# Token layer of a four-layer convolution network: a chunk's pieces in another order, its means in another PSUM bank

## The chip, the cores and the metric

The kernel runs on one core of a Trainium2 chip. The metric is the device time of one launch in microseconds; the median of three runs is 7043.77 us (7041.89 to 7046.84). The core has five engines that work side by side, each through its own queue of instructions in order: TensorE (PE; its weight loads are listed as PEld), VectorE (DVE), ScalarE (ACT), GpSimd (POOL) and SyncE (SP), which mostly issues DMAs. TensorE writes its products to PSUM, which has eight banks.

## The reference, cut to what matters

The input x has shape (4, 48, 256, 256). Four residual layers follow each other; each first normalizes x in 16 groups of channels (`_gn`) and adds its result to x.

```
x = x + L0(_gn(x))   # channel attention: 1x1 and 3x3 depthwise convolutions, softmax over 48x48, projection
x = x + L1(_gn(x))   # the token layer
x = x + L2(_gn(x))   # scans with a 5-tap convolution: down, up, right, left
x = x + L3(_gn(x))   # the same with other weights
```

The token layer reads the normalized image as tokens of 48 numbers, by a plain reshape of memory:

```
t = x.reshape(B, H * W, dim)
t = gelu(gelu(t @ W1 + b1))               # 48 -> 16, exact gelu, twice
x1, x2 = t[..., :8], t[..., 8:]
n = layernorm(x2)                         # mean and variance over 8 numbers
sp = depthwise3x3(n) + dw_b;  ch = conv1x1(n) + pw_b     # n as an image with 8 channels
g = x1 * (sp * ch)
out = g @ W2 + b2                         # 8 -> 48
```

## The kernel before, in words

`layers01` computes layers 0 and 1, `scans` layers 2 and 3. In `layers01` a first stage sums the products from which the attention of each image is made. Then the output of layer 0 is computed in blocks of 16 rows, 16 blocks an image. `block(u)` has six pieces, three to a half block: two calls of `full` (three matmuls each) and one of `rest` (six matmuls on two halves of the rows at once). Half block 0 takes the parts c = 0 and 2, half block 1 the parts 1 and 3. `rest` ends with two additions on VectorE (L720) and two `bn_stats` (L721), which collect the statistics for the next normalization; at half block 1 it also lets ScalarE normalize the next block's input (x1n and x2n, L654). The function `conv` runs one half block.

The 16 blocks of image 0 run alone. The remaining 96 half blocks share the engines with the token layer: four of them run first, and then `tick(c, conv, alone)` (L1040) is called once for each step of the token layer, which is cut into 32 chunks of 32 rows (eight an image). A tick holds four half blocks and pieces of three chunks: the transposes of chunk c + 1, the hidden layer and the norm of chunk c, gate and output of chunk c - 2. When no half blocks are left, `alone` is true and the ticks hold token work only; that is so from chunk 22 on. In the text these are lone ticks, the others mixed ticks.

The pieces of a chunk, in the order in which its data needs them:

- `load` and `relay` (L860, L867): the tokens come by DMA (tok), and GpSimd rearranges them in two copies (pairs).
- `transposed` (L873): six pieces, each four transposes on TensorE into one bank and a copy out of it (xt), by VectorE for even pieces and ScalarE for odd ones.
- `hidden` (L820, L890 to L901): two groups of eight matmuls, each into one bank, and the gelus on ScalarE.
- `centered` (L907 to L911): a matmul gives the mean in every row (pm), VectorE subtracts it (d), GpSimd squares (sq).
- `normed` (L916 to L942): a matmul gives the variance (pvar); ScalarE takes the root, VectorE the reciprocal (L919) and the product (L921), ScalarE writes n (L923). Four small DMAs on ScalarE's queue then carry border rows: two of the chunk itself (L933, L934), one into the border tile of the chunk before (L938), one into that of the chunk after (L942). At an image's first or last chunk one of them carries zeros.
- `shift` and `gate` (L946 to L961): GpSimd copies the border tile three times, shifted (nears). TensorE makes the depthwise convolution (psp): three matmuls from n (L952) and one from the border copies (L953); another matmul makes the pointwise convolution (pch, L955). ScalarE and VectorE combine the two (sp), GpSimd multiplies (g).
- `output` (L991 to L1006): for each of two parts ip, four matmuls into four banks (pout), eight additions of the residual on VectorE (L1001) into y, eight copies on GpSimd into yr. `finish` takes four `bn_stats` of y (L1034). One DMA pair writes yr to memory for the scans (x2r, L1018).

The PSUM banks are five in the pool `banks`, two in `spare` and one in `p_small`. The tiles of `banks` are handed out in rotation: a tile waits until the fifth tile before it has been read. Half block 0 uses `spare`, half block 1 `banks`; everything else named above uses `banks`.

The program is written with a tile framework: the Python code gives an order of pieces, and a planner with estimated costs puts the instructions of each engine's queue in an order that may differ from it a little. On each engine the built order is kept at run time. In a mixed tick of the kernel before, TensorE's built order is: mean, two of the six transposing pieces, projections of part 0, half block 1, two transposing pieces, variance, projections of part 1, half block 0, two transposing pieces, half block 1, hidden layer of the next chunk, gate, half block 0.

## Time and profile before

| what | us |
|---|---|
| median of three runs | 7043.77 |
| the profiled execution, its own time | 7044.79 |
| span of its instructions | 7042.9 |
| first mean of a chunk / mean of chunk 22 / mean of chunk 31 (start) | 1221.8 / 2323.9 / 2614.5 |
| first work of the scans | 2697.2 |
| one mixed tick without a disturbance, 1406.4 to 1456.2 | 49.8 |

| busy in the whole span | us |
|---|---|
| TensorE matmuls | 6623.6 |
| VectorE | 3630.5 |
| GpSimd | 2085.2 |
| ScalarE | 1854.1 |

A row of the timeline has the start, the time until the group's last instruction ends, the engine (with a q when it is the engine's queue issuing a DMA), the line, the operation, out<-in, and how often; in square brackets the idle time of the engine before it and what ended it. Matmuls of 32-bit numbers stand as two records each. A busy TensorE can contain waits that are shorter than a record, so the distance from one group's start to the next is the better measure. The granted clock is the share of TensorE's full clock.

### The profile page before, as it was taken

Reading aid. Unit: us, or ns where it says so; the run is one execution under the profiler, and the core shown is the slowest. Engines: PE = TensorE matmul, PEld = TensorE weight load, DVE = VectorE, ACT = ScalarE, POOL = GpSimd, SP = SyncE. Lnnn points to the kernel's source line nnn. Section 1 sums busy time; section 2 is a strip of 40 time slices with the busy share of each in tenths; the row PEclk is TensorE's granted clock in tenths of the full one; section 3 lists DMA queues with packets and bytes.
Section 4 is the critical chain, followed back from the end, with each engine's and each line's share of the span. In section 5 each row is a group of like instructions: output and inputs, shape, how many; then the busy total and the mean of one; then the engine's idle time right before and its main releaser. Section 6 shows DMA issues by size and latency. Waiting matters only on the chain.

```text
span 7042.9 us, 133633 instructions
## 1 busy us (share of the span) xinstructions
PE 6623.6 (94%) x55772; PEld 5308.8 (75%) x55772; DVE 3630.5 (52%) x8740; ACT 1854.1 (26%) x2166; POOL 2085.2 (30%) x4211
## 2 busy tenths in 40 slices
PE   6999999999999767999998999986898999899999
PEld 5666533333333226999998999986798999899999
DVE  7777533455555554444444446754344444444444
ACT  3430022434344443453431000001444444000000
POOL 0000000233333454330003556762000000455777
PEclk9999999999999888999999999998899999999999
DMA  7742145666666667994677777989997466865775
GB/s 233 183 133 83 62 142 165 180 176 186 182 190 185 158 156 218 294 282 122 207 210 186 202 185 174 253 241 196 179 170 126 140 191 182 227 191 173 275 292 202
DMA packets 1177470, 1326.23 MB, mean 188 GB/s; under 512 B 831040, under 2 KB 1005760, under 8 KB 1124512
## 3 DMA queue, kind: packets, MB, share of 16 engines
q1 hardware_dynamic: 1163696, 1229.16, 64.3%
q10 hardware_dynamic: 13072, 88.18, 3.7%
q8 instruction: 438, 7.18, 0.4%
q14 instruction: 168, 1.38, 0.1%
q0 software_dynamic: 96, 0.33, 0.0%
HBM read 794.28 MB, written 522.19 MB: 187 GB/s over the span
## 4 chain that ended last, share of the span: by engine, by line
PE 56%; SPq 3%; DMA 3%; DVE 2%; POOL 1%; issue 1%; ACT 1%; ACTq 0%; POOLq 0%; DVEq 0%
PE ps L1206 55%; SPq L1242 3%; DMA D<-d 1%; ACT d L1281 1%; POOL s L1491 1%; DMA near<-n 0%; DMA tok<-x 0%; DVE y L1001 0%; DVE v L919 0%; POOL yr L1006 0%; DVE st L1034 0%; DMA r<-R 0%; DMA x2r<-yr 0%; PE ptok L873 0%; PE ph L820 0%
## 5 line engine op out<-in xcount | busy, mean ns | idle before, releaser
L1206 PE MATMUL ps<-d,w 128*128 128x128 f32 (+1 forms) x18360 | 2075.3, 277 | 107.7 <-DVE d L1212 69.4
L1206 PEld LDWEIGHTS ps<-d,w 128*128 128x128 f32 x18360 | 2070.6, 193 | 112.3 <-DVE d L1212 73.0
L1206 PE MATMUL ps<-r,w 128*128 128x128 f32 (+1 forms) x18360 | 2066.5, 276 | 69.8 <-POOL r L1423 36.5
L1206 PEld LDWEIGHTS ps<-r,w 128*128 128x128 f32 x18360 | 2064.2, 193 | 72.1 <-POOL r L1423 37.4
L1212 DVE SCALAR_TENSOR_TENSOR d<-ps,b,d 128x128 f32<-128x128 f32 x3054 | 978.6, 348 | 1166.1 <-PE ps L1206 1080.3
L1491 POOL TENSOR_TENSOR s<-s,r 128x128 f32<-128x128 f32 x1536 | 748.3, 528 | 330.3 <-DVE r L1212 327.8
L1212 DVE SCALAR_TENSOR_TENSOR r<-ps,b,pre 128x128 f32<-128x128 f32 x1530 | 490.4, 348 | 578.9 <-PE ps L1206 569.2
L1212 DVE SCALAR_TENSOR_TENSOR r<-ps,b,r 128x128 f32<-128x128 f32 x1530 | 489.2, 347 | 458.8 <-PE ps L1206 430.5
L374 PE MATMUL acc<-moving,raw 128*32 128x240 f32 (+1 forms) x6144 | 688.9, 382 | 12.2 <-DVE moving L357 11.5
L697 PE MATMUL py<-x1n,wy 128*96 128x512 f32 x1536 | 696.7, 602 | 1.9
L1423 POOL COPY pre<-c 128x128 f32<-128x128 f32 x1530 | 559.5, 405 | 464.7 <-DVE r L1212 463.7
L374 PE MATMUL acc<-moving,still 128*32 128x240 f32 (+1 forms) x6144 | 685.5, 382 | 6.0 <-DVE still L361 2.2
L1281 ACT ACTIVATE d<-x,spread 128x256 f32<-128x256 f32 x752 | 510.6, 826 | 555.5 <-DMA D<-d 343.5
L1362 ACT COPY u<-d 128x384 f32<-128x384 f32 x510 | 452.0, 903 | 569.9 <-DVE d L1212 509.4
L374 PEld LDWEIGHTS acc<-moving,raw 128*32 128x32 f32 x6144 | 434.9, 110 | 197.6 <-DVE moving L357 11.8
L697 PEld LDWEIGHTS py<-x1n,wy 128*96 128x96 f32 x1536 | 243.7, 164 | 415.1 <-issue 373.4
L1423 POOL COPY r<-c 128x128 f32<-128x128 f32 x6 | 2.4, 396 | 1700.1 <-DMA c<-U 1700.1
L720 DVE TENSOR_TENSOR y<-py,t 96x512 f32<-96x512 f32 x256 | 173.3, 677 | 559.6 <-PE py L706 559.6
L374 PEld LDWEIGHTS acc<-moving,still 128*32 128x32 f32 x6144 | 361.2, 110 | 37.0 <-issue 5.8
L1006 POOL COPY yr<-y 96x256 f32<-96x256 f32 x512 | 316.1, 660 | 202.0 <-DVE y L1001 191.8
L706 PE MATMUL py<-x2n,wy 64*96 64x512 f32 x1536 | 362.5, 604 | 0.0
L706 PEld LDWEIGHTS py<-x2n,wy 64*96 64x96 f32 x1536 | 117.0, 159 | 234.4 <-issue 229.5
(219 smaller groups left out, 4173.9 us busy)
## 6 DMA issues: line engine op xcount, KB each, us to landing
t<-in_xc SPq DMA_DIRECT2D x64, 1536.0 KB
c<-U SPq DMA_DIRECT2D x348, 256.0 KB
D<-d SPq DMA_DIRECT2D x54, 1536.0 KB
d<-D SPq DMA_DIRECT2D x54, 1536.0 KB
R<-r SPq DMA_DIRECT2D x54, 1536.0 KB
r<-R ACTq DMA_DIRECT2D x54, 1536.0 KB
U<-u SPq DMA_DIRECT2D x84, 768.0 KB
raw<-in_xp SPq DMA_DIRECT2D x36, 1728.0 KB
```

The source lines that it names most:

```text
L374: nc.tensor.matmul(out[32 * i : 32 * i + 32, : n * C], lhsT=still[i][:, first : first + 32], rhs=moving[:, i, lo : lo + n * C], start=u == ...
L697: nc.tensor.matmul(ps, lhsT=held["w"][0][:, dx], rhs=x1n[:, 2 * c : 2 * c + 2, dx : dx + W], start=dx == 0, stop=False)
L706: nc.tensor.matmul(held["ps"][q + 2 * s], lhsT=held["w"][1][here, dx], rhs=x2n[here, 2 * q : 2 * q + 2, dx : dx + W], start=False, stop=dx ...
L720: nc.vector.tensor_add(part, held["ps"][c], t1[:P, 2 * c : 2 * c + 2, :])
L1006: nc.gpsimd.tensor_copy(yrs[c][:, :, 2 * i2 + ip, :].rearrange("p j (n a g) -> p j n a g", a=4, g=4)[:, :, :, al], y[:, i2, al].rearrange( ...
L1206: nc.tensor.matmul(ps[m][:, here], lhsT=w[:, n, :], rhs=old[:, q, there], start=first, stop=last)
L1212: nc.vector.scalar_tensor_tensor(new[:, m], ps[m], bias[:, m : m + 1], inp[:, m], ALU.add, ALU.add)
L1242: queues[q % len(queues)].dma_start(v[p0 : p0 + np_, m, 8 * n0 : 8 * n1], src[c0:c1, 8 * n0 : 8 * n1, at : at + 64])
L1281: pin(nc.scalar.activation(dst, src, AF.Identity, bias=g[:, 1:2], scale=g[:, 0:1]))
L1362: nc.scalar.copy(v[:, :, i, :, al], line)
L1423: nc.gpsimd.tensor_copy(dst[:, m].rearrange("p (J a b) -> p J a b", J=NBK, b=B), v[:, m, j, :, gl].rearrange("p J b a -> p J a b"),)
L1491: nc.gpsimd.tensor_add(v, v, line[:, m].rearrange("p (J a b) -> p J a b", J=NBK, b=B))
```

## The change

In `layers01`, the `bn_stats` of a half block are put into a list and issued at the start of the next half block. The pool `big` and the pool `spare` are handed to `gated_layer`. The mean and the variance (pm, pvar) of a chunk are made in the bank of `p_small`. `normed` is split: the root stays in it, the reciprocal, the product, n and the border DMAs become `scaled`. `output` is split in two pieces of two projections each; in lone ticks the second and fourth projection use `spare`, and y of part 1 has its own buffers in `big`. In lone ticks the DMA of yr is issued in the tick's last piece instead of right after the output.

The pieces of a tick have a new order. In mixed ticks the six transposing pieces stand together behind the second half block, and the variance stands behind the third. TensorE's built order there is: mean, projections of part 0, half block 1, six transposing pieces, half block 0, variance, projections of part 1, half block 1, hidden layer of the next chunk, gate, half block 0. In lone ticks the gate comes after four transposing pieces rather than at the start, and both parts of the output come last.

On ScalarE the built order of a mixed tick has n, the normalization of x1n, and then the four border DMAs; before, the border DMAs followed n directly. On GpSimd, in lone ticks, the border copies of chunk c - 1 stand in tick c: in ticks 25, 27 and 29 ahead of the pairs copies, in ticks 26, 28 and 30 ahead of the yr copies; before, they stood at the start of tick c + 1. On SyncE, the load of tok for every second lone chunk stands behind the four loads of xr.

```
@@ -674,6 +674,7 @@
     stats = {}
     ends = []
     unwritten = []
+    behind = []
 
     def block(u):
 
@@ -683,6 +684,9 @@
         held = {}
 
         def full(c):
+            if c < 2:
+                while behind:
+                    behind.pop(0)()
             if c == 0:
                 if u + 1 < len(items):
                     ahead_[u + 1] = load(items[u + 1])
@@ -718,9 +722,15 @@
             for c in (q, q + 2):
                 part = held["y"][:, 2 * c : 2 * c + 2, :]
                 nc.vector.tensor_add(part, held["ps"][c], t1[:P, 2 * c : 2 * c + 2, :])
-                nc.vector.bn_stats(stats[b][:, n * 4 + c, :], part.rearrange("p h w -> p (h w)"))
+                behind.append(
+                    lambda c=c, part=part: nc.vector.bn_stats(
+                        stats[b][:, n * 4 + c, :], part.rearrange("p h w -> p (h w)")
+                    )
+                )
             if q == 0:
                 return
+            while behind and n == NB - 1:
+                behind.pop(0)()
             dst = x1[b].rearrange("c (h w) -> c h w", w=W)
 
             def write(y=held["y"]):
@@ -746,7 +756,7 @@
         some_late()
     sctx.close()
 
-    tick, n_ticks = gated(ctx, tc, banks, p_small)
+    tick, n_ticks = gated(ctx, tc, banks, p_small, big)
     todo = [(u, q) for u in range(NB, len(items)) for q in range(2)]
     made = {}
 
@@ -768,7 +778,7 @@
             piece()
 
 
-def gated_layer(ctx, tc, banks, p_small, x1, x2r, w1, w2, dw, ends, pw, cols, b2, k, coef1, coef2):
+def gated_layer(ctx, tc, banks, p_small, big, spare, x1, x2r, w1, w2, dw, ends, pw, cols, b2, k, coef1, coef2):
 
 
 
@@ -902,7 +912,7 @@
             h2s[c] = h
 
     def centered(c):
-        pm = banks.tile([128, CH], F32, tag="bank", name="pm")
+        pm = p_small.tile([128, CH], F32, tag="small", name="pm")
         h2 = h2s.pop(c)
         nc.tensor.matmul(pm, lhsT=k["mean8", 128], rhs=h2, start=True, stop=True)
         d = ds[c] = feat.tile([128, CH], F32, tag="d", name="d")
@@ -910,12 +920,18 @@
         sq = sqs[c] = feat.tile([128, CH], F32, tag="sq", name="sq", bufs=1)
         nc.gpsimd.tensor_mul(sq, d, d)
 
+    vs = {}
+
     def normed(c):
-        b, j = items[c]
-        pv = banks.tile([128, CH], F32, tag="bank", name="pvar")
+        pv = p_small.tile([128, CH], F32, tag="small", name="pvar")
         nc.tensor.matmul(pv, lhsT=k["mean8", 128], rhs=sqs.pop(c), start=True, stop=True)
         v = feat.tile([128, CH], F32, tag="v", name="v", bufs=1)
         nc.scalar.activation(v, pv, AF.Sqrt, bias=eps)
+        vs[c] = v
+
+    def scaled(c):
+        b, j = items[c]
+        v = vs.pop(c)
         nc.vector.reciprocal(v, v)
         d = ds.pop(c)
         nc.vector.tensor_mul(d, d, v)
@@ -975,30 +991,35 @@
         t = xrs[c, ip]
         nc.scalar.activation(t, t, AF.Identity, bias=b2_sb)
 
-    def output(c, ip, alone):
+    def output(c, ip, i, alone):
         b, j = items[c]
-        if ip == 0:
+        if ip == 0 and i == 0:
 
             yrs[c] = res.tile([P, 8, 4, 128], F32, tag="yr", name="yr")
             if j == 0:
                 stats[b] = feat.tile([P, NJ * 8, 6], F32, tag="st", name="st1")
-        y = ys[c, ip] = res.tile([P, 2, 4, W], F32, tag="y1", name="y1")
-        t, g = xrs[c, ip], gs[c]
-        ps = []
-        for q in range(4):
-            p = banks.tile([P, 2, W], F32, tag="bank", name="pout")
+        if i == 0:
+            if alone and ip:
+                ys[c, ip] = big.tile([P, 2, 4, W], F32, tag="y", name="y1", bufs=2)
+            else:
+                ys[c, ip] = res.tile([P, 2, 4, W], F32, tag="y1", name="y1")
+        y, t, g = ys[c, ip], xrs[c, ip], gs[c]
+        ps = {}
+        for q in (2 * i, 2 * i + 1):
+            ps[q] = (spare if alone and q % 2 else banks).tile([P, 2, W], F32, tag="bank", name="pout")
             here = slice(32 * q, 32 * q + 32)
             nc.tensor.matmul(
-                p,
+                ps[q],
                 lhsT=w2_sb[here, ip, :],
                 rhs=g[here],
                 start=True,
                 stop=True,
             )
-            ps.append(p)
-        for q in range(4):
+        for q in ps:
             for kk in range(2):
                 nc.vector.tensor_add(y[:, q % 2, 2 * kk + q // 2, :], ps[q][:, kk], t[:, 4 * kk + q, :])
+        if i == 0:
+            return
         if alone:
             load_x(c + 1, ip)
         for i2 in range(2):
@@ -1021,8 +1042,6 @@
                 )
 
         unwritten.append(write)
-        if alone:
-            unwritten.pop()()
 
     after = []
     unwritten = []
@@ -1062,36 +1081,30 @@
         def last():
             if c + 2 < n:
                 load(c + 2)
+            while alone and unwritten:
+                unwritten.pop(0)()
 
         pieces = [first]
         if now:
             if items[c][1] == 0:
                 pieces.append(lambda: strips(items[c][0]))
             pieces += [lambda: hidden(c, 1), lambda: hidden(c, 0)]
-        if was:
-            pieces.append(lambda: gate(old))
-        pieces.append(conv)
-        if now:
-            pieces.append(lambda: centered(c))
-        if new:
-            pieces += [lambda i=i: transposed(c + 1, i) for i in range(2)]
-        if was:
-            pieces += [lambda: [add_b2(old, ip) for ip in range(2)], lambda: output(old, 0, alone)]
-        pieces.append(conv)
-        if new:
-            pieces += [lambda i=i: transposed(c + 1, i) for i in range(2, 4)]
-        if was:
-            pieces.append(lambda: finish(old, 0))
-        if now:
-            pieces.append(lambda: normed(c))
-        if was:
-            pieces.append(lambda: output(old, 1, alone))
-        pieces.append(conv)
-        if new:
-            pieces += [lambda i=i: transposed(c + 1, i) for i in range(4, NI)]
-        if was:
-            pieces.append(lambda: finish(old, 1))
-        pieces += [conv, last]
+        turned = lambda *which: [lambda i=i: transposed(c + 1, i) for i in which] if new else []
+        out = lambda ip: [lambda i=i: output(old, ip, i, alone) for i in range(2)] if was else []
+        of_now = lambda f: [lambda: f(c)] if now else []
+        of_old = lambda f, *more: [lambda: f(old, *more)] if was else []
+        added = of_old(lambda c: [add_b2(c, ip) for ip in range(2)])
+        if alone:
+            pieces += [conv] + turned(0, 1) + of_now(centered) + turned(3) + of_old(gate) + added
+            pieces += turned(4) + of_now(normed) + turned(2, 5) + of_now(scaled)
+            pieces += out(0) + of_old(finish, 0) + out(1) + of_old(finish, 1)
+        else:
+            pieces += of_old(gate)
+            pieces += [*added, conv, *of_now(centered), *out(0), conv]
+            pieces += turned(0, 1, 3, 4, 2, 5) + of_old(finish, 0)
+            pieces += [conv, *of_now(normed), *out(1), conv]
+            pieces += of_now(scaled) + of_old(finish, 1)
+        pieces.append(last)
         if c == n + 1:
             pieces.append(lambda: [piece() for piece in unwritten + after])
         return pieces
@@ -1612,10 +1625,10 @@
     x1 = [dram.tile([C, HW], F32, tag=f"x1_{b}", name=f"x1_{b}") for b in range(B)]
     x2r = [dram.tile([8 * C, 8, 1024], F32, tag=f"x2r_{b}", name=f"x2r_{b}") for b in range(B)]
 
-    def gated(ctx, tc, banks, p_small):
+    def gated(ctx, tc, banks, p_small, big):
         names = ("w1", "w2", "dw", "ends", "pw", "cols", "b2")
         to = [coef2[:, b] for b in range(B)]
-        return gated_layer(ctx, tc, banks, p_small, x1, x2r, *(a[n] for n in names), k, coefs[1], to)
+        return gated_layer(ctx, tc, banks, p_small, big, spare, x1, x2r, *(a[n] for n in names), k, coefs[1], to)
 
     names = ("wqk", "dwqk", "wv", "dwv", "projT", "temp")
     layers01(tc, a["x"], a["xp"], a["xe"], a["inside"], a["pick"], a["rows"], a["xc"], x1, *(a[n] for n in names), k, coefs[0], coefs[1], gated, spare)
```

## The prediction

> **What bounds the kernel now.** I first read the busy time by stretch, for a stretch in which half blocks and token chunks alternate (a "mixed tick", clean one of 49.80 us) and for the stretch with chunks alone ("lone ticks", chunks 22 to 30). Columns: window, length, busy time of PE, PEld, DVE, ACT, POOL, granted clock, DMA share, GB/s.
>
> ```profile
> 1406.40:1456.20 49.80, 49.70 (x185) 18.73 (x183) 27.34 (x47) 20.52 (x20) 17.40 (x31) 1.00 0.70 191
> 2324.00:2614.50 290.50, 198.47 (x786) 78.47 (x786) 160.88 (x298) 127.49 (x147) 148.07 (x205) 0.80 0.72 168
> ```
>
> A mixed tick is TensorE's: 49.70 of 49.80 us. In the lone stretch no engine is full (TensorE 198 of 290.5 us, at 0.80 of the clock), so chains of waits set it. There are 20 full mixed ticks (chunks 2 to 21) and 9 lone ones; the scans after 2697 us, more than half of the run, are not touched.
>
> A busy TensorE can hide waits for banks inside a group, so next I read the timeline of that tick (start, duration, engine):
>
> ```profile
> 1419.35 1.02 PE L916 MATMUL pvar<-sq,cst 128*128 128x512 f32 x2
> ...
> 1420.30 2.98 PE L991 MATMUL pout<-g,w_sb 32*96 32x512 f32 x8
> ...
> 1424.17 3.35 DVE L919 RECIPROCAL v<-v 128x512 f32<-128x512 f32 x1 [1.14 <-ACT v L918]
> ...
> 1428.43 1.34 ACT L923 ACTIVATE n<-d,col 128x512 f32<-128x512 f32 x1 [4.29 <-DVE d L921]
> ...
> 1431.15 0.63 ACTq L938 DMA_DIRECT2D near<-n  x1
> ...
> 1437.78 1.90 POOL L946 COPY nears<-near 16x512 f32<-16x512 f32 x3 [7.10 <-DMA near<-n]
> ...
> 1446.46 1.02 PE L953 MATMUL psp<-nears,ends_sb 80*128 80x512 f32 x2
> ```
>
> Two things are to be seen. The four projections (pout) take 2.98 us here and 1.92 us at 1408.33; from start to next start 2.93 and 2.02 us. In the lone ticks, with banks free, the same eight records take 1.04 us (2353.5 us). The answer on the tile pout names what they wait for, 20 times each in the mixed stage (us in total, times):
>
> ```profile
>   ACT xt L877: 15.7, 20
>   DVE st L721: 15.2, 20
>   DVE d L909: 11.5, 20
> ```
>
> These are copies of transposes, the bn_stats ahead of an addition, and the reader of the mean: bank tenants. Second, a chain starts at pvar: square root, reciprocal, n, four small DMAs of border rows, the border copy (nears) on GpSimd, and only then the last tap of the gate (L953). GpSimd waited 7.10 us for the DMA. TensorE came 27.11 us after pvar's start, the copy had ended at 20.33 us: 6.8 us of slack. Over the chunks of the mixed stage whose border copy needs its successor (17 of them) the copy ends 19.9 to 23.9 us after pvar, mean 21.8; its slack is 3.3 to 9.4 us.
>
> **The change part by part, mixed ticks.** The order that the build gives each engine is read beside the diff.
>
> Projections: all four banks are free in both places, since the means leave the rotation and eight microseconds of half block pass after the transposes. Gain (2.02 - 1.04) + (2.93 - 1.04) = 2.87 us a tick.
>
> Six transposes together: 24 instructions, 2.83 us as before (0.97 + 0.93 + 0.93). Six banks are wanted of five, two just left by a half block. Its additions end 0.79 and 2.1 us after it (0.69 + bn_stats 0.61 + 0.67); the fifth transposition would start at 1.86, the sixth at 2.6 and needs the first one's copy, at 2.8 us. Cost 0.5 us.
>
> Means in the one small bank: pm and pvar of a chunk are a conv or more apart and read within 3 us. Nothing; in lone ticks they follow each other and must wait for each other's data anyway. Deferred bn_stats: VectorE is busy 27.3 of 49.8 us, so 1.3 us later hides in its idle time; without that cover each bn_stats is 0.6 us. The half block's two DMAs (t in, x out) are issued as before.
>
> Variance: it moves behind the third half block instead of the second. n depends on it, and so does the border copy of the chunk before, which the next tick's gate reads. From pvar to the last tap TensorE had 0.95 + 2.91 + 8.07 + 0.93 + 8.0 + 3.57 + 2.68 = 27.1 us; now 0.95 + 1.04 + 8.05 + 3.57 + 2.68 = 16.3 us. The chain does not get shorter: VectorE now has two additions and two bn_stats of the half block (2.5 us), four additions of y (1.4), the reciprocal (3.3), four more (1.4), d*v (0.7): n ends at 10.7 us (10.4 before). On ScalarE the activation of x1n (2.10 us, at 1415.83) now stands between n and the DMAs, so the third, decisive one is issued at 15 us instead of 12.4 us. If it lands as late after its issue as before, the copy ends at 21.8 + 2.4 = 24.2 us; if the burst of xr and x2r transfers beside it sets the landing, some 2 us sooner. I take 23.5: a wait of 7.2 us at L953. Behind it stand pch and the whole next half block; nobody on TensorE can go past.
>
> *Rule against row, landing.* The Trainium skill (DMA: Bandwidth & Descriptors, Anatomy of one DMA) gives a fixed cost of about 2 us for a DMA, fitted on another issuing path; 8.1 KB adds nothing. Then the copy would end at 15 + 2 + 1.9 = 18.9 and the wait be 2.6 us. The trace says 3.7 to 9.5 us from the end of the third issue to the copy's start in mixed ticks (6.0 in the tick shown). The measurement decides.
>
> *Rule against row, clock.* Its TensorE: Matmul & The Clock Gate (HAM oscillation) holds that idle gaps over some 3.4 us drop the clock to half. The trace agrees with a number: TensorE waited 3.74 us for a group norm until 1505.42, and then
>
> ```profile
> 1500.50:1505.40 4.90, 1.18 (x3) 0.16 (x1) 2.38 (x5) 3.60 (x5) 1.26 (x1) 1.00 0.43 111
> 1505.50:1509.60 4.10, 4.10 (x8) 1.54 (x9) 0.60 (x4) 0.26 (x1) 0.00 (x0) 0.58 1.11 216
> ```
>
> 0.58 over 4.10 us is 1.7 us of work lost. The same happened after the other 3.7 us wait, not after one of 1.67 us. So each 7.2 us wait costs 1.7 us more (0.9 to 2.5). The page's Part 4 adds that transposes don't count as activity; 2.83 us of them is below the window, so I take nothing; at worst 1.7 us a tick.
>
> Sum of a mixed tick: -2.87 + 0.5 + 7.2 + 1.7 = +6.5 us. Gates of 20 chunks fall into full mixed ticks; two of them are a batch's last chunk, whose lower border is zero and waits for nobody. 18 x 6.5 - 2 x 2.4 = **+112 us**.
>
> **Lone ticks.** Before, they last 27.0, 29.3, 41.5, 28.3, 35.1, 29.1, 34.8, 27.9 and 37.5 us from mean to mean (290.6). In the new order two kinds alternate. In chunks 25, 27, 29 pvar stands right behind pm, and on GpSimd the border copy that needs this very chunk's n is queued ahead of the pairs copy, hence of all transposes. Chain: d 0.7, square 1.0, pvar 1.0, root 0.7, reciprocal 3.3, product 0.7, n 1.3 with hops 9.2; third DMA issued at 11.2; landing 4.5 (4.0 to 4.9 in chunks 24 to 28); copy 1.9; pairs 2.9: 20.5. Then a transposition and the gate, 0.6 + 4.4; multiply and g 2.1; projections 1.0: 28.6. Sixteen additions and eight bn_stats on VectorE, 2 x (2.73 + 2.46) = 10.4: **39 us**. In 26, 28, 30 VectorE needs 26 us, but the border copy stands ahead of the 16 yr copies (2 x 4.7), so GpSimd is free for the next square only at **34 us**. Three pairs 219 us; chunks 22 to 24, where these copies block less, 28 + 33 + 26 = 87. Together 306, that is +15, and 3 us a pair for half clock: **+25 us**. Bounds: -84 if VectorE's own work sets them, +60 if pairs or xr land late (SP issues the tok loads behind the four xr loads). The last two ticks and the first scan loads follow one chain before and after (yr, x2r, additions): 0, within 10 us.
>
> Total +137 on the profiled execution, 7044.79 us with a span of 7042.9 (1.9 us lie around it): 7182. The median shown is 1.0 us below that execution, so **7181 us**, 2% slower.
>
> **Rivals.**
> A, faster: the lone ticks become VectorE's. Its work in one is 3 x 0.68 + 0.69 + 3.34 + 0.68 + 0.75 + 5.46 + 4.92 = 17.9 us; with 3.1 us of waiting for the variance 21, so 9 x 11.3 = -102 us. For: no engine was full there. Against: the queue order on GpSimd above. It decides once the border wait is under some 6.5 us a tick; at the shortest landing seen (3.7 us: wait 4.3) mixed ticks cost +61 and the time is 7003 us.
> B: the 2 us landing. Wait 2.6 us, no clock loss: 18 x 0.75 - 5 = +9, with +25 lone 7078 us. For: the small size. Against: every mixed row.
> C: the change doesn't free the banks, the projections still take 4.9 us a tick: 20 x 2.87 = +57, 7238 us. Against: their tenants are named and gone.
>
> **How the numbers follow.** Forecast 0.67, A 0.12, B 0.11, C 0.10. The forecast's own range is 7110 to 7245: wait 5.5 to 8.5 (-30, +24), clock (±15), lone -40 to +35. To hold 8 in 10 the range goes down to B: 7070 to 7245. Within 0.2% (14 us, about what a measurement of this kernel can tell from no change) lies only an edge of A and B, 0.03; faster 0.11; slower 0.86.
>
> **What would show it.** Right: projections near 1.04 us in both places of a mixed tick; a wait of 5 to 8 us of L969's matmul for nears on GpSimd in 18 ticks, mixed ticks of 55 to 58 us, half clock after it; lone ticks alternating about 40 and 34. Wrong: no TensorE idle ahead of that tap (the DMA lands early), or lone ticks near 22 us, or projections still of 2 to 3 us.

## Result and profile after

The changed kernel takes 7154.79 us (median of 5 runs, 7148.66 to 7161.75) against 7046.84 us before (5 runs, 7041.89 to 7054.98): ratio 1.0154, 95% interval 1.0139 to 1.0169. It is 1.5% slower; the forecast was 7181 us. The profiled execution took 7160.22 us, its span is 7158.4 us, 115.5 us longer than the span before. Cut by the mean matmul (pm) of the chunks, the difference lies here:

| stage | before | after | difference | forecast |
|---|---|---|---|---|
| start to the mean of chunk 22 (mixed) | 2323.9 | 2425.6 | +101.7 | +112 |
| lone ticks, chunks 22 to 30 | 290.5 | 291.6 | +1.1 | +25 |
| chunk 31 to the end | 4428.4 | 4441.2 | +12.8 | 0 |

First the busy time by stretch: one mixed tick without a group norm, from mean to mean, and the lone stage (columns as before).

```profile
1429.70:1486.70 57.00, 50.44 (x185) 18.54 (x183) 27.42 (x47) 20.12 (x20) 17.77 (x31) 0.94 0.61 167
2425.60:2717.20 291.60, 187.75 (x762) 73.71 (x762) 156.64 (x289) 125.73 (x143) 134.58 (x186) 0.77 0.57 131
```

The mixed tick has 57.00 us instead of 49.80, and TensorE is busy in 50.44 of them. It idles now, and its clock is 0.94 on the average. The timeline of this tick shows where (only the chain of the variance, and what goes out on the two transfer queues beside it):

```profile
1451.08 1.12 PE L927 MATMUL pvar<-sq,cst 128*128 128x512 f32 x2
...
1452.13 1.11 PE L1011 MATMUL pout<-g,w_sb 32*96 32x512 f32 x8
...
1459.81 0.82 SPq L988 DMA_DIRECT2D xr<-x  x2
...
1460.46 1.36 ACT L939 ACTIVATE n<-d,col 128x512 f32<-128x512 f32 x1 [7.54 <-DVE d L937]
...
1461.59 2.07 ACT L654 ACTIVATE x1n<-t,g 128x2048 f32<-128x2048 f32 x1
...
1461.85 0.63 ACTq L949 DMA_DIRECT2D near<-n  x1
...
1462.17 2.42 SPq L1039 DMA_DIRECT2D x2r<-yr  x2
...
1463.18 3.18 ACTq L954 DMA_DIRECT2D near<-n  x1
...
1472.08 1.89 POOL L962 COPY nears<-near 16x512 f32<-16x512 f32 x3 [9.78 <-DMA near<-n]
...
1474.03 2.07 PE L969 MATMUL psp<-nears,ends_sb 80*128 80x512 f32 x2 [6.37 <-POOL nears L962]
```

The projections (pout) take 1.11 us where they took 2.98. TensorE reaches the last gate tap 16.6 us after the variance's matmul and stands there for 6.37 us, because the border copy on GpSimd waits 9.78 us for the border DMA. Two things in these lines were not in the forecast. The decisive third DMA (L954) needs 3.18 us to be issued, where before it took 0.63. And x1n does not stand in its way: the first border DMA goes out at 1461.85, while x1n runs (1461.59 to 1463.66). (The 2.42 us of the row x2r are two requests of 0.30 us with a wait for the landing of xr between them.)

In the kernel before, x2r was requested beside the border DMAs too, but later against them, 0.45 us ahead of the third one (1431.15, shown with the prediction):

```profile
1430.70 4.60 SPq L1018 DMA_DIRECT2D x2r<-yr  x2
...
1431.81 3.60 ACTq L942 DMA_DIRECT2D near<-n  x1
```

There (again two requests of 0.30 us in the first row) the long issue fell on the fourth border DMA, which this tick's gate does not need; the third took 0.63 to 0.65 us in every mixed tick. In the changed kernel x2r goes out 1.0 us ahead of the third, and the third takes 2.69 to 3.66 us (chunks 2 to 20).

What TensorE waits for in the mixed stage, by sum, times and longest (us):

```profile
PE psp L969 <- POOL nears L962: 93.9, 16, 8.5
PE pg L94 <- DVE mv L1056: 7.1, 2, 3.6
```

Before, the first of these waits was not there. And the tile pout: of the three reasons shown before (15.7, 15.2 and 11.5 us, 20 times each) none is left; its idle time in the mixed stage is

```profile
  issue: 25.8, 34
  DVE y L724: 3.0, 4
```

Last, the clock of the shown tick behind the wait, from the tap to the next mean:

```profile
1474.00:1486.70 12.70, 12.67 (x29) 4.55 (x29) 0.75 (x1) 7.05 (x9) 1.26 (x1) 0.77 0.25 93
```

A granted clock of 0.77 over 12.70 us is 2.9 us of work lost (0.23 x 12.70), beside the 6.37 us of idle time.

### The profile page after: what moved, and what is told of

Same layout as the page of the kernel before. It is cut to its first block, busy times and chain, and to the rows that moved or that the text cites. A ratio compares the mean times of both kernels' runs of the same rounds, so it can differ in the third digit from the quotient of the medians.

```text
span 7158.4 us, 133533 instructions
## 1 busy us (share of the span) xinstructions
PE 6620.6 (92%) x55772; PEld 5305.2 (74%) x55772; DVE 3627.1 (51%) x8740; ACT 1844.8 (26%) x2166; POOL 2086.0 (29%) x4211
## 4 chain that ended last, share of the span: by engine, by line
PE 79%; DVE 5%; DMA 5%; SPq 3%; POOL 3%; issue 2%; ACT 1%; ACTq 0%; POOLq 0%; DVEq 0%
PE ps L1219 53%; PE py L701 8%; PE acc L374 8%; PE py L710 4%; SPq L1255 3%; DMA near<-n 2%; POOL yr L1027 1%; DVE v L935 1%; DMA D<-d 1%; DVE y L1020 1%; DVE y L724 1%; POOL s L1504 1%; POOL nears L962 1%; ACT d L1294 1%; PE psp L969 1%
## 5 line engine op out<-in xcount | busy, mean ns | idle before, releaser
L374 PE MATMUL acc<-moving,raw 128*32 128x240 f32 (+1 forms) x6144 | 686.8, 381 | 12.4 <-DVE moving L357 11.5
```

The source lines that it names most:

```text
L374: nc.tensor.matmul(out[32 * i : 32 * i + 32, : n * C], lhsT=still[i][:, first : first + 32], rhs=moving[:, i, lo : lo + n * C], start=u == ...
```

## Experiments

The theory: the late variance makes the border transfer late, the gate waits for it, and the wait lowers the clock. Its rivals: the new order (transposes in one group, banks) is slow by itself; the excess is the wait alone; the transfer is late for another reason than its late place on ScalarE. Ratios are against the kernel before in the same session; the changed kernel has 1.0154. Where a stage is given, it is cut as in the table above.

**1. Variance early, all else as changed.**

```diff
-            pieces += turned(0, 1, 3, 4, 2, 5) + of_old(finish, 0)
-            pieces += [conv, *of_now(normed), *out(1), conv]
-            pieces += of_now(scaled) + of_old(finish, 1)
+            pieces += of_now(normed) + turned(0, 1, 3, 4, 2, 5) + of_now(scaled) + of_old(finish, 0)
+            pieces += [conv, *out(1), conv]
+            pieces += of_old(finish, 1)
```

> The changed kernel, with one thing moved in the mixed ticks: the variance's matmul goes behind the second half block, ahead of the six transposes, and the scaling with its four border DMAs behind the transposes; the lone ticks stay as changed. If the wait at the last gate tap, with the half clock behind it, is the whole loss of the mixed stage (prediction's cause): every mixed tick should cost what the two ticks without a neighbour wait cost in the changed kernel, 47.5 us. The excess over 47.5 us in its ticks sums to about 165 us, so 7155 - 165 = 6990 us (6975 to 7020), no idle at that tap, and TensorE at full clock. If the loss lies in the new order itself (transposes in one group, banks), and the wait only shows it: 7100 us or more. If the earlier scaling delays the additions on VectorE or the copies on ScalarE in turn: 7020 to 7080 us, with a new wait named in front of the transposes or the fourth half block.

Measured: 7003.16 us (6994.79 to 7011.99), ratio 0.9944 (0.9923 to 0.9965): faster than before. Chunk 22 is reached at 2262.6 us, 163 us sooner than in the changed kernel. An ordinary tick from its busy times by stretch:

```profile
1354.20:1401.40 47.20, 47.04 (x184) 17.74 (x182) 27.52 (x47) 20.42 (x20) 16.86 (x31) 1.00 0.76 201
```

No idle time, clock 1.00, 47.20 us. So the new order is a gain of 2.6 us a tick as long as the variance is early; the place of the variance is the whole loss, and more. (The time is 13 us above what was expected: the lone stage came out at 305.7 us, see 6.)

**2. Variance late, all else as before.**

```diff
         pieces.append(conv)
+        if now and not alone:
+            pieces.append(lambda: normed(c))
         if new:
             pieces += [lambda i=i: transposed(c + 1, i) for i in range(4, NI)]
         if was:
             pieces.append(lambda: finish(old, 1))
-        pieces += [conv, last]
+        pieces.append(conv)
+        if now and not alone:
+            pieces.append(lambda: scaled(c))
+        pieces.append(last)
```

> The kernel before, with only this moved in its mixed ticks: the variance's matmul goes behind the third half block, the scaling and its border DMAs behind the fourth; transposes, banks and lone ticks are those of before. If the place of the variance alone makes the loss: each of some 17 mixed ticks gains a wait of about 6.5 us at the last gate tap and 2 to 3 us of half clock, 17 x 9 = 153 us, so 7045 + 153 = about 7198 us (7150 to 7240). If the grouping of the transposes or the banks is needed for the loss: within 20 us of 7045 us.

Measured: 7140.94 us (7138.62 to 7143.64), ratio 1.0138 (1.0122 to 1.0153). The place alone makes a loss of the same kind, in ticks that keep the old transposes and banks; it is two thirds of what was expected. The timeline of an ordinary tick shows how it differs:

```profile
1390.15 1.13 PE L918 MATMUL pvar<-sq,cst 128*128 128x512 f32 x2
...
1399.47 1.37 ACT L930 ACTIVATE n<-d,col 128x512 f32<-128x512 f32 x1
...
1402.16 0.35 SPq L648 DMA_DIRECT2D t<-in_xc  x1
1402.21 0.64 ACTq L945 DMA_DIRECT2D near<-n  x1
...
1409.00 1.89 POOL L953 COPY nears<-near 16x512 f32<-16x512 f32 x3 [8.62 <-DMA near<-n]
1410.94 2.07 PE L960 MATMUL psp<-nears,ends_sb 80*128 80x512 f32 x2 [4.55 <-POOL nears L953]
```

Here the third border DMA is issued in 0.64 us and is out 12.7 us after the variance; no x2r goes out beside it, its requests came some 15 us earlier. The wait is 4.55 us instead of 6.4. It is no shorter because the landing is still late: 6.15 us from the end of the issue to the copy (1402.85 to 1409.00), 5.9 to 6.5 us in the ordinary ticks. Here the half block's load t (1.5 MB) was requested 0.05 us ahead of the border DMA, its two stores and the loads of tok just behind; which of these holds it up was not tried, but it is not x2r. And fewer ticks pay in full: where a batch's group norm already stops TensorE, the waits overlap (chunk 5: 57.5 us before, 58.4 here).

**3. Border DMAs ahead of x1n.** The scaling goes before the fourth half block, and this half block's x1n is held behind the DMAs on ScalarE.

```diff
-            pieces += [conv, *of_now(normed), *out(1), conv]
-            pieces += of_now(scaled) + of_old(finish, 1)
+            pieces += [conv, *of_now(normed), *out(1), *of_now(scaled)]
+            pieces += [lambda: BEHIND.append(1), conv, BEHIND.clear]
+            pieces += of_old(finish, 1)
...
-        nc.scalar.activation(v[:, :, 1 : W + 1], t, AF.Identity, bias=g[:, 1:2], scale=g[:, 0:1])
+        made = nc.scalar.activation(v[:, :, 1 : W + 1], t, AF.Identity, bias=g[:, 1:2], scale=g[:, 0:1])
+        if BEHIND:
+            tc.keep_in_program_order(made)
```

> The changed kernel, with the mixed ticks' four border DMAs put ahead of the normalization copy x1n on ScalarE's queue (x1n is held behind them); all else as changed. If the landing follows the issue: the third DMA goes out 2.1 us earlier, the wait shrinks from 6.3 to about 4.2 us, 17 x 2.1 = 36 us, about 7119 us (7100 to 7130). If the landing is set by the load of the DMA queues instead, or x1n, now later, stalls the next half block: within 10 us of 7155 us, or slower.

Measured: 7154.13 us (7148.07 to 7160.13), ratio 1.0156 (1.0140 to 1.0173): nothing. An ordinary tick takes 56.5 us on the average against 56.9; the 2.1 us of the forecast for x1n don't exist. The timeline:

```profile
1398.11 0.82 SPq L993 DMA_DIRECT2D xr<-x  x2
1398.76 1.36 ACT L944 ACTIVATE n<-d,col 128x512 f32<-128x512 f32 x1 [7.53 <-DVE d L942]
1400.14 0.63 ACTq L954 DMA_DIRECT2D near<-n  x1
1400.46 0.88 SPq L1044 DMA_DIRECT2D x2r<-yr  x2
...
1401.48 2.78 ACTq L959 DMA_DIRECT2D near<-n  x1
...
1406.93 2.10 ACT L654 ACTIVATE x1n<-t,g 128x2048 f32<-128x2048 f32 x1 [6.82 <-PE psp L973]
1410.08 1.90 POOL L967 COPY nears<-near 16x512 f32<-16x512 f32 x3 [9.56 <-issue]
1412.03 2.08 PE L974 MATMUL psp<-nears,ends_sb 80*128 80x512 f32 x2 [6.07 <-POOL nears L967]
```

x1n now comes last, and the third DMA still takes 2.78 us to be issued and is out 14.9 us after the variance (1389.37 to 1404.26). Just ahead of it SyncE has requested two xr and two x2r transfers.

**4. The store of x2r behind the first half block's transfers.** In the mixed ticks only.

```diff
-            while unwritten:
-                unwritten.pop(0)()
+            if alone or todo_none:
+                write_out()
...
-            pieces += [*added, conv, *of_now(centered), *out(0), conv]
+            pieces += [*added, conv, write_out, *of_now(centered), *out(0), conv]
```

(`write_out` empties the same list and holds both requests where they are written; `todo_none` is true in the first ticks and the last.)

> The changed kernel, with the store of the previous chunk's result (x2r, two transfers of 0.79 MB) requested behind the first half block's transfers (t in, x1 out) in every mixed tick, instead of at the tick's start, where in the changed kernel it goes out 0.3 to 1 us ahead of the border DMAs. In the changed kernel and with x1n moved out of the way alike, the first two border DMAs take 0.63 us to issue and the third 2.8 to 3.2 us. If that transfer's backlog is what holds the third issue and its landing: the issue takes 0.6 us, the third DMA is out at 12.7 us after the variance, lands within 4.5 us, the wait at the gate falls to 2.6 us or less and the half clock goes: 17 x (3.7 + 2.8) = 110 us faster than changed, about 7045 us (7010 to 7115). If the border DMAs' lateness has nothing to do with x2r: 7145 to 7165 us.

Measured: 7028.35 us (7022.83 to 7031.76), ratio 0.9976 (0.9966 to 0.9985). One store moved on SyncE's queue takes back more than the whole loss. The timeline:

```profile
1391.59 0.82 SPq L988 DMA_DIRECT2D xr<-x  x2
1392.24 1.37 ACT L939 ACTIVATE n<-d,col 128x512 f32<-128x512 f32 x1 [7.53 <-DVE d L937]
...
1394.98 0.63 ACTq L954 DMA_DIRECT2D near<-n  x1
...
1397.91 1.90 POOL L962 COPY nears<-near 16x512 f32<-16x512 f32 x3 [3.82 <-DMA near<-n]
1398.16 2.69 SPq L1039 DMA_DIRECT2D x2r<-yr  x2
1399.86 1.13 PE L969 MATMUL psp<-nears,ends_sb 80*128 80x512 f32 x2 [0.42 <-POOL nears L962]
```

The third border DMA is issued in 0.63 us at 12.7 us after the variance, as the forecast had it without x1n, and lands 2.30 us later (1395.61 to 1397.91) where it took 5.7 us in the changed tick (1466.36 to 1472.08). The wait is 0.42 us. So of the 6.37 us, about 2.5 us were the issue held up, and 3.4 us the landing behind 1.57 MB of x2r. The variance is as late here as in the changed kernel: its late place takes the cover away, and the transfers requested ahead of the border DMA make that cover needed. Take away either of the two and the mixed ticks have no loss (an ordinary one 48.20 us here, 47.20 in experiment 1).

**5. The clock by itself.** Matmuls that nobody reads fill the wait; the results are unchanged. Nine of them, first, in the small bank between the third tap and the border tap; then seven in the gate's own bank ahead of its first tap:

```diff
         for dx in range(3):
+            if dx == 0 and warm:
+                for _ in range(7):
+                    tap = nc.tensor.matmul(psp, lhsT=dw_sb[:, 1, :], rhs=n[:, :, 1 : W + 1], start=True, stop=True)
+                    tc.keep_in_program_order(tap)
             nc.tensor.matmul(psp, lhsT=dw_sb[:, dx, :], rhs=n[:, :, dx : dx + W], start=dx == 0, stop=False)
```

> The changed kernel, with nine more matmuls (128 x 512, 0.59 us each, 5.3 us) in every mixed tick that has a neighbour to wait for, between the three full taps and the border tap; they go to the small bank and nothing reads them, so the result is unchanged. They fill the wait, which itself stays, since its cause (the late border transfer) stays. If the gap lowers TensorE's clock afterwards, at 2 to 3 us a tick: 17 x 2.5 = 43 us faster than the changed kernel, about 7112 us (7095 to 7130), and the half-clock stretches behind the tap gone. If the excess over the wait is not the clock but something else behind the late gate (ScalarE, VectorE): same as changed, 7150 to 7165 us.

> The changed kernel, with seven more matmuls (128 x 512, 0.59 us each, 4.1 us) in each mixed tick with a neighbour, put ahead of the gate's three full taps into the gate's own bank, which the first tap then overwrites: the result is unchanged, no other bank is touched. TensorE is then idle for about 2 us instead of 6.3 us in front of the border tap, and the tap itself starts when it did. With nine such matmuls in the small bank the clock stayed full, the undisturbed ticks were 1.6 us shorter although the tap came 1.2 us later, and four ticks with a group norm lost 6 us each to the shared bank. If the clock is a loss of its own of 2.8 us a tick: 17 x 2.8 = 48 us faster than changed, about 7107 us (7090 to 7125). If what was won there came from elsewhere: within 10 us of 7155 us.

Measured: 7168.35 us, ratio 1.0177 (1.0162 to 1.0193) with nine, 7147.68 us, ratio 1.0148 (1.0132 to 1.0164) with seven. By the total this misses (7112 and 7107 expected); the ticks tell it apart. An ordinary tick with seven:

```profile
1368.00:1422.20 54.20, 53.58 (x198) 20.19 (x196) 27.42 (x47) 20.12 (x20) 17.80 (x31) 1.00 0.65 176
```

The clock is 1.00, and over the eleven ordinary ticks (chunks 2 to 4, 6, 10 to 12, 14, 18 to 20) the mean is 54.1 us against 56.9 in the changed kernel: 2.8 us, as expected, at an unchanged start of the tap (22.9 us after the variance). In chunks 5, 9, 13 and 17 the ticks are 4.8 to 6.9 us longer than in the changed kernel. In 9 and 17 TensorE has its idle time at the group norm and had none left at the tap, so the seven matmuls are pure work. In 5 and 13 the group norm's second matmul, which stands behind the tap, now waits 6.27 us; why is open. With nine matmuls the same four ticks lose 3.6 to 7.9 us, so the loss there does not need the shared bank that the second expectation blames. The clock is a loss of its own, then, and filling the wait is no remedy here.

**6. The stages apart.** The changed mixed ticks with the lone ticks' order of before, and the reverse. In both, the means are in the small bank throughout:

```diff
         if alone:
-            pieces += [conv] + turned(0, 1) + of_now(centered) + turned(3) + of_old(gate) + added
-            pieces += turned(4) + of_now(normed) + turned(2, 5) + of_now(scaled)
-            pieces += out(0) + of_old(finish, 0) + out(1) + of_old(finish, 1)
+            pieces += of_old(gate) + [conv] + of_now(centered) + turned(0, 1) + added + out(0)
+            pieces += [conv] + turned(2, 3) + of_old(finish, 0) + of_now(normed) + of_now(scaled)
+            pieces += out(1) + [conv] + turned(4, 5) + of_old(finish, 1) + [conv]
```

> The changed order in the mixed ticks, with the lone ticks' order, banks, buffers and the time of their stores as before; the means in the small bank throughout. From the two traces the mixed stage alone is worth +101.7 us, the lone stage +1.0 and the passage to the scans +9.6: 7045 + 102 = about 7147 us (7135 to 7160) if stages add up. The prediction had 7045 + 112 = 7157 us here. If the lone ticks of before, starting later against their transfers, answer with gains or losses of their own: outside that range.

> The mixed ticks' order of before (variance behind the second half block, transposes in pairs), with the lone ticks as changed, the means in the small bank and the half blocks' bn_stats deferred. Prediction: +25 us for lone ticks, nothing at the end: 7070 us. From the two traces: +1 for the lone stage and +10 for the passage to the scans: 7056 us, less up to 2.9 us a tick (57 us) where the means' freed banks alone shorten the projections. If the lone ticks' new order costs what was seen behind the mixed stage with the early variance (306 against 292 us): 7070 us as well.

Then the kernel before with the small bank for the means and nothing else, and the early variance of experiment 1 with lone ticks wholly as before, means in the rotating banks included:

> The kernel before with one thing changed: the two means of a chunk (pm, pvar) get the small bank instead of the rotating ones; order, transposes, bn_stats and lone ticks as before. The run with only the lone ticks changed had mixed ticks of 48.5 us instead of 49.8, so the freed banks should give about 1.3 us in some 19 ticks, 25 us; the run with only the mixed ticks changed had a lone stage of 311 us with the order of before, the run with the means back in the rotation 285 us, so one bank for both means should cost some 20 us in the lone ticks. Together within 15 us of before (7025 to 7050 us), with chunk 22 at about 2300 us instead of 2324 and a lone stage of about 310 us. If the small bank costs nothing in lone ticks, as the prediction had it: about 7017 us, lone stage 285 to 292 us.

> The changed mixed ticks with the variance behind the second half block, and the lone ticks entirely as before (order, means in the rotating banks, four result banks from the rotation, stores at once). The mixed stage of the first should reach chunk 22 at 2263 us as in the run with the early variance; from there to the end before had 4719 us, the changed kernel 4733 us and the early variance with changed lone ticks 4734 us. If stages add up: 2263 + 4719 + 2 = about 6984 us (6972 to 6998), faster than every other version. If the lone ticks' cost follows from where their transfers stand at the start and not from their order: 6995 to 7010 us.

| kernel | time us | ratio | chunk 22 at | lone stage | from 22 to the end |
|---|---|---|---|---|---|
| before | | 1 | 2323.9 | 290.5 | 4719 |
| changed | 7154.79 | 1.0154 | 2425.6 | 291.6 | 4733 |
| mixed only | 7165.06 | 1.0167 (1.0149 to 1.0184) | 2427.1 | 311.1 | 4738 |
| lone only | 7033.79 | 0.9987 (0.9980 to 0.9994) | 2303.2 | 301.5 | 4732 |
| small bank only | 7053.74 | 1.0011 (1.0002 to 1.0020) | 2310.6 | 310.1 | 4742 |
| early variance, lone changed | 7003.16 | 0.9944 (0.9923 to 0.9965) | 2262.6 | 305.7 | 4735 |
| early variance, lone as before | 6985.29 | 0.9922 (0.9907 to 0.9937) | 2260.9 | 285.4 | 4721 |

Three readings. The mixed order is the loss, with either lone order. The changed lone ticks cost about 14 us more than those of before from chunk 22 to the end in these two pairs; over all kernels here that differ only ahead of chunk 22 it is 11 us (seven with the changed lone ticks 4721 to 4735 us, mean 4730; three with those of before 4717 to 4721). How much of it shows in the lone stage and how much after it depends on whether the alternation of short and long ticks ends on a short one (20.4 us in the changed kernel) or a long one (51.8 with the early variance), so the sum is the number to use. And the small bank for both means, which the forecast had at nothing, costs some 20 us in the lone ticks' old order (310.1 against 290.5), and wins 1.1 us in most ordinary mixed ticks (48.7 to 48.8 against 49.8). Which wait costs the 20 us is not shown; that of the transposes for pairs grew from 34.5 to 50.7 us. "Mixed only" missed its expectation by this, and "small bank only" ended 4 us above its range. Whether the small bank also costs in the new lone order was not tried.

**7. The border copies behind pairs on GpSimd, in the lone ticks.**

```diff
-            nc.gpsimd.tensor_copy(shifted[c % 2][32 * dx : 32 * dx + 2 * F], near[c % NN][:, :, dx : dx + W])
+            made = nc.gpsimd.tensor_copy(
+                shifted[c % 2][32 * dx : 32 * dx + 2 * F], near[c % NN][:, :, dx : dx + W]
+            )
+            if behind:
+                tc.keep_in_program_order(made)
```

> The changed kernel, with GpSimd's queue in the lone ticks re-ordered: the three border copies (nears) are held behind the two copies into pairs that all transposes wait for. In the changed kernel's long lone ticks the border copy stands ahead of pairs and waits for its transfer (nears ends at 2525.8 us, pairs follow until 2528.7), in the short ones it stands ahead of the sixteen yr copies (nears ends at 2574.5). The prediction made this queue order the cause of its 39 and 34 us ticks. If it is: 3 to 5 us less in each of four long ticks and some in the short ones, the lone stage 291.6 - 25 = about 267 us (255 to 280), the time 7155 - 25 = about 7130 us. If the lone ticks are set elsewhere (VectorE, the tok transfers): lone stage 285 to 300 us, the time within 10 us of 7155 us; if the square of the next chunk, now behind a border copy in the short ticks, waits in its turn: slower.

Measured: 7111.90 us (7108.20 to 7125.04), ratio 1.0106 (1.0090 to 1.0121), lone stage 254.2 us (in the profiled execution, which took 7125 us). GpSimd's waits in the lone stage, the changed kernel first (us in all, times, longest):

```profile
POOL nears L962 <- DMA near<-n: 61.1, 6, 12.8
...
POOL pairs L877 <- DMA tok<-x: 2.0, 1, 2.0
```

and with the new queue order:

```profile
POOL g L981 <- DVE sp L979: 40.9, 9, 6.6
POOL pairs L877 <- DMA tok<-x: 29.2, 4, 9.0
```

61.1 us of waiting for the border DMA are gone; half of it comes back as pairs waiting for its own data, and the lone stage is 37 us shorter. So the queue order on GpSimd makes 37 of the 292 us: the long ticks 25, 27 and 29 take 34.4 to 43.8 us instead of 45.8 to 52.7. The alternation itself stays (the short ticks still take 20.4 to 23.1 us), so it has another cause as well.

**8. Early variance and pairs first.**

> The changed kernel with both: the variance behind the second half block in the mixed ticks, and in the lone ticks the border copies behind the copies into pairs. Mixed stage as in the run with the early variance (chunk 22 at 2263 us). If GpSimd's queue order sets the lone ticks: 7003 - 25 = about 6978 us. If not: 6995 to 7010 us.

Measured: 6955.70 us (6953.28 to 6965.33), ratio 0.9884 (0.9867 to 0.9900); lone stage 265.3 us. It beats both kernels: 1.2% faster than before, about 2.7% faster than the change as it stands (0.9884 / 1.0154 = 0.973).

## Why the prediction was right, and where it was not

The sign, the place and the mechanism of the mixed ticks (a late border transfer, a wait at the tap, half clock behind it) were right, and the size within 26 us, in part by luck, since errors of its terms balance. Step by step:

- *Projections, -2.87 us a tick.* Right: 1.05 us at both places. The two ticks whose gate waits for nobody show the tick without the wait: 47.5 us in chunks 8 and 16; the forecast's own terms give 49.80 - 2.87 + 0.5 = 47.4. Rival C falls.
- *Six transposes together, +0.5.* Right: 3.25 us from first to next start in chunk 5, 3.33 forecast.
- *Deferred bn_stats, nothing.* n ends 10.7 us after the variance's matmul, as forecast with them counted in.
- *TensorE at the tap 16.3 us after the variance.* Right: 16.6 us in the shown tick.
- *x1n between n and the DMAs, 2.1 us.* This step failed. The third DMA was out at 15.3 us, forecast 15, but experiment 3 takes x1n away and nothing moves, and experiment 4 takes x2r away and 2.6 us of issue are gone. Right number by coincidence, wrong cause: the fault was to count an activation as work that a DMA behind it must wait for. Here the requests go out while the activation runs.
- *The landing.* The forecast took 8.5 us from issue to the end of the copy (15 to 23.5) and named "the burst of xr and x2r transfers" only as a reason for an earlier end. In the changed kernel that burst was the cause of the lateness: with x2r out of the way the DMA lands in 2.3 us. The fixed cost of about 2 us that the Trainium skill gives for another issuing path (DMA: Bandwidth & Descriptors, Anatomy of one DMA) is thus near the 2.3 us of experiment 4, where x2r is not requested ahead; beside a half block's load and stores it was 6.15 us again (experiment 2). The rows of 3.7 to 9.5 us that the forecast preferred had x2r just ahead as well. Preferring the row was right for the changed kernel, since the store was there.
- *Wait 7.2 us.* 6.3 in the ordinary ticks: over-sized by 0.9.
- *Half clock 1.7 us (0.9 to 2.5).* Under-sized: 2.9 us by the clock's row, 2.8 by experiment 5. It had been scaled from one wait of 3.74 us; one of 6.4 us is followed by a longer slow stretch. Nor do idle gaps tell the whole clock: in the kernel before, three more slow stretches of 3.4 us (clock 0.51 from 1581.2, 2045.4 and 2096.6) stand behind projections that waited for their banks, with no gap of TensorE over 0.2 us there.
- *18 ticks.* Over-counted: 15 of the 18 have the wait (the sixteenth in the list is in chunk 1's tick, which the forecast did not count). In chunks 9 and 17 a group norm's wait stands ahead of the gate and covers the border transfer, and in chunk 21, the last, TensorE comes to the tap late by itself. In other ticks with a group norm, that norm had cost before what the border wait costs now (chunk 5: 57.5 us before, 56.2 after). An ordinary tick is 6.9 us longer, the six with a group norm or a new batch (5, 7, 9, 13, 15, 17) 2.2 us on the average. The errors of wait, clock and count balance by luck: +101.7 for +112.
- *Means in the small bank, nothing.* Right in mixed ticks. Wrong in the lone ticks' old order by about 20 us; why the reason given for it, that they must wait for each other's data anyway, does not hold there is open.
- *Lone ticks, +25 us.* Over-sized: +1.1, with the passage to the end +13.9, and 11 to 14 in the comparison of experiment 6. The mechanism, GpSimd's queue, is shown by experiment 7 for 37 us of the long ticks. The split was wrong: 45.8 to 52.7 and 20.4 to 23.0 us instead of 39 and 34. A pair takes 66.7 to 73.1 us (forecast 73, and 3 for the clock).
- *The last ticks and scan loads, 0 within 10.* 12.8 us in this execution, 0.4 with the early variance; it is the other half of the alternation and belongs with the lone ticks.

Rival A needed a border wait below 6.5 us and lone ticks at VectorE's pace. The wait was there (6.3), the pace was not: VectorE is busy in 156.64 of 291.60 us. Rival B, a landing of 2 us, is what experiment 4 makes of the kernel: it had 7078 us, with 25 us of lone ticks that didn't come; measured 7028.

## What to carry to other kernels

When a producer is moved later, measure from its new place to the consumer how much work still lies between, and set it against the whole chain, the small transfer included: here 10.8 us of cover were given away, and the freed banks did not need it (47.20 us a tick with the early variance). The landing of the small transfer was made here by what was requested just ahead of it on another queue, so look at the large loads and stores that go out in the same microseconds before blaming the engine's own queue, and move them. The idle gap on TensorE was charged twice, 6.3 us as waiting and 2.8 us as clock; and a wait counts only in those rounds in which no other wait already covers it.

## What the runs showed of the hardware

A request for about 8 KB on ScalarE's queue took 2.69 to 3.66 us to issue, not 0.63, when the store x2r (two requests of 0.79 MB) had begun to go out on SyncE's queue about 1.0 us before, and landed 5.7 us after its issue in the shown tick instead of 2.3. Requested 0.4 to 0.5 us behind the first x2r request, in the kernel before, it took 0.63 to 0.65 us, and the next one took 2.8 to 4.9 us in 15 of 17 ticks. SyncE's own request t took 2.06 us in the shown tick, 0.35 us in experiment 4. A late landing did not need a long issue: 6.15 us beside t and the half block's stores in experiment 2, with an issue of 0.64 us. The Trainium skill's Perfetto Trace Analysis (DMA Instruction — HWDGE (DVE, Sync)) describes a descriptor generator shared by two issuing sequencers, and a reported time that includes the wait for its lock; the rows fit, but no run here separates that lock from full queues behind it.
